# Projecting a tile one tile (one block) behind its transposes, in a four-layer graph network

## The chip, the cores and the metric

The kernel runs on one core of a Trainium2 chip. The metric is the device time of one execution in microseconds (us); smaller is better. A core has engines that each work through their own instructions in order and wait for one another through semaphores: PE (TensorE: matmuls; its weight loads are listed apart as PEld), ACT (ScalarE), DVE (VectorE) and POOL (GpSimd), and SP (SyncE), which here issues the DMAs.

## What is computed

A graph of 3327 nodes with 256 features each goes through four layers, each of the form x = x + layer(relu(layernorm(x)), adj). All data are float32. Layer 0 (two steps of attention with a top-p cut) is not touched by the change. Layers 1 to 3 are, cut to what matters:

```python
# layer 1
filt = tanh(adj * adj) * (adj > 0)               # the largest 700 of a row; rows here have fewer
x = x + relu(filt @ (tanh(h @ W_proj + b_proj) @ W_gcn) + b_gcn)
# layer 2
h = maximum(layernorm(x), 0)
Wh = h @ W
e = leaky_relu((Wh @ a[:256])[:, None] + (Wh @ a[256:])[None, :], 0.2)
x = x + softmax(where((adj > 0) | eye, e, -9e15), axis=1) @ Wh
# layer 3: the same with its own W and a, without eye, and elu around the product
```

Layer 2 so needs, for every node, the projection Wh of the normalized output of layer 1, and the two scores of Wh with the halves of a; layer 3 needs the same of layer 2's output.

## The kernel before

The 3327 nodes are padded to 26 tiles of 128 rows (NT = 26). A float32 product of two 128-row operands is two matmul instructions in the profile.

**Layer 1** is a loop over the tiles `it`. For each, the 26 blocks of the transposed adjacency come by DMA in two halves of 13 (`blk`, three tiles deep), DVE makes max(a, 0) * a in place (L1472), ACT the tanh in place (L1473), and PE multiplies the blocks with `gw`, 26 products that add up in a half of the PSUM tile `ps_wide` (L1476). One iteration later `summed(it - 1)` adds the bias, takes the relu and adds the residual on DVE (L1454, L1455; two tiles share one `ps_wide` and are done as a pair), and takes the layernorm statistics (L131 and L132 on DVE; L792, L793 and L1388 on POOL: adding epsilon, a power of -1/2, the product for the bias). Another iteration later `entered2(it - 2)` brings the tile into layer 2 by `Entry.tile_in`:

- ACT writes the normalized tile `hr` (L1394),
- PE transposes it in two halves into a `ps_row` (L785) and ACT copies that to `ht` (L786),
- PE multiplies `ht` with the weights and the two vectors made of them and `a` (L1399), into another `ps_row`,
- ACT copies the two scores to `sd` (L1403) and the rest to `wh` (L1404).

After the last tile of a span (four tiles; `ends`), `spread` transposes the scores of the span to a row (L1416, in a `ps_row`), ACT adds the `shift` and stores it in `dk` (L1419), POOL scales the scores (L1420), and DVE takes the largest of them for the first four rows of tiles (L1423). In the same iteration the rows of the adjacency of tile `it` come by DMA (`adj_rows`, L1488), DVE marks the positive ones in `pos` (L1490), POOL clears the padding (L1493), and SP stores it (L1494).

**Layers 2 and 3** are the function `attention`. It goes over seven spans of four tiles (the last has two) and, inside, over seven blocks `b` of four columns of tiles, two columns at a time: four exponentials on ACT (L1579, L1580), their maximum and the masking on DVE (L1581, L1582), and four tiles' products on PE (L1588). In blocks 1 to 4 the maximum over the next span's rows is taken (L1595), then turned into rows for the exponentials by transposes (L1535) and copies (L1538). At a span's end `finish` divides and adds the residual (L1611, L1629). The span's tiles enter layer 3 in the blocks of the next span: `todo` holds a list of work for each block, statistics two tiles ahead, then `tile_in`, and after the fourth tile the `spread`. For layer 3, `tile_in` also adds `wh` to `part` on POOL (L1407).

**What sets the order.** The program is written in the order of the loops; a scheduler then places each engine's instructions, and may move an instruction past others of the same engine. Buffers bound it: `hr` and `ht` have two, and `ps_row` has two for everything that uses it, taken in turn: transposes, projections, spreads, the rows of scores and the small product of `shift`. A new user of a `ps_row` waits until the one before the last has been copied out.

`Entry.__init__` also makes `shift` and `low` for its layer at once: DVE squares a column of weights (L1368), PE sums it with a matmul of ones (L1370), DVE (L1374) and POOL (L1375 to L1379) finish it. `entry2` is made before layer 1, `entry3` before layer 2.

Of the kernel before, what the change touches and what calls it, by code (L numbers as in the profile page):

```python
# [66 lines left out]
def kernel(  # L67
# [678 lines left out]
    def layers(fast):  # L746
# [606 lines left out]
        class Entry:  # L1353
# [5 lines left out]
            def __init__(self, name, w, wh, dk_tag, eye):  # L1359
                self.w, self.wh, self.eye, self.mv = w, wh, eye, {}  # L1360
                for t in wh.halves:
                    nc.gpsimd.memset(t[:, :, D : D + 1], 1.0)
                self.sd = late.tile([P, NT, 2], F32, name=f"sd{name}")
                self.d2 = late.tile([P, NT], F32, name=f"d2{name}")
                self.dk = slot(dk_tag, [P, NP], f"dk{name}")
                self.tops = late.tile([P, 4, len(spans)], F32, name=f"tops{name}")
                sq = late.tile([P, 2], F32, tag="sq", name="sq")
                nc.vector.tensor_tensor(sq, w[:, :, D + 1], w[:, :, D + 1], ALU.mult)  # L1368
                ps = ps_row()
                nc.tensor.matmul(ps[:, :2], ones, sq, start=True, stop=True)  # L1370
                self.shift = late.tile([P, 1], F32, name=f"shift{name}")
                self.low = late.tile([P, 1], F32, name=f"low{name}")
                shift = self.shift
                nc.vector.tensor_reduce(shift, ps[:, :2], AX.X, ALU.add)  # L1374
                nc.gpsimd.tensor_scalar(shift, shift, 1.01 * D, EPS, ALU.mult, ALU.add)  # L1375
                nc.gpsimd.tensor_tensor(shift, shift, half, ALU.pow)
                nc.gpsimd.tensor_scalar(shift, shift, 1.0, None, ALU.add)

                nc.gpsimd.tensor_scalar(self.low, shift, -1.0 + 2.0**-20, None, ALU.mult)  # L1379
                if not eye:  # L1380

                    self.part = late.tile([P, D + 1], F32, name="part")
                    nc.gpsimd.memset(self.part, 0.0)

# [5 lines left out]

            def tile_in(self, it, src):
                hr = late.tile([P, D], F32, tag="hr", bufs=2, name="hr")
                mv = self.mv.pop(it)
                nc.scalar.activation(hr, src, AF.Relu, bias=mv[:, 0:1], scale=mv[:, 1:2])  # L1394
                ht = late.tile([P, D], F32, tag="ht", bufs=2, name="ht")
                transposed(hr, ht)
                ps = ps_row()
# [49 lines left out]
        with tc.tile_pool(name="l1", bufs=2, reuse_waits="tile") as l1:  # L1447
# [9 lines left out]

            def entered2(it):
                entry2.tile_in(it, xn(it))
                if it in ends:  # L1460
                    entry2.spread(ends.index(it))

            for it in range(NT):
# [17 lines left out]
                if it >= 2:  # L1481
                    entered2(it - 2)
                ar = slot(f"e{it % 2}", [P, NP], "adj_rows")
# [11 lines left out]
            summed(NT - 1)  # L1495
            entered2(NT - 2)
            entered2(NT - 1)


# [10 lines left out]
        def attention(entry, finish, following=None):  # L1510
# [33 lines left out]
            for i, span in enumerate(spans):  # L1544
# [16 lines left out]
                for b, j0 in enumerate(range(0, NT, JB)):  # L1561
# [30 lines left out]
                    if 1 <= b <= len(ahead):  # L1592
# [6 lines left out]
                        if b == len(ahead):  # L1599
                            sb_next = scores_of(ahead, top)  # L1600
                    if b and todo:
                        for work in todo.pop(0):
                            work()
# [10 lines left out]
                if following is not None:  # L1614

                    stats = [lambda it=it: following.stats(it, xn(it)) for it in span]
                    rest = [lambda it=it: following.tile_in(it, xn(it)) for it in span]
                    todo += [stats[:2]] + [rest[k : k + 1] + stats[k + 2 : k + 3] for k in range(n)]
                    todo.append([lambda i=i: following.spread(i)])
            for works in todo:  # L1620
# [108 lines left out]
```

## Time and the profile before

| | us |
|---|---|
| three runs | 3114.98, 3118.21, 3117.26 |
| their median | 3117.26 |
| the profiled execution | 3111.67 |
| its span, first to last instruction | 3109.9 |
| layer 1's products (L1476), first and last start | 1998.1, 2351.4 |
| the products of layers 2 and 3 (L1588), first and last start | 2379.2, 3099.2 |
| stretch of layer 3, 2772 to 3100: PE, DVE, ACT busy of 328 | 316.90, 290.74, 243.73 |

Times in a timeline are microseconds from the start of the span; a group such as "x4" is four instructions in a row with the time from the first's start to the last's end. What stands in brackets at the end of a line is how long the engine stood idle before it, and the instruction that ended the wait. In the list of waits the columns are who waited for whom, the total in us, how often, and the longest. The mean granted PE clock of the execution is 0.973 of full speed.

### The profile page before, as it was taken

What the parts mean: (1) busy time and instruction counts of PE and PEld (TensorE: products, weight loads), DVE (VectorE), ACT (ScalarE), POOL (GpSimd) and SP (SyncE); (2) the same over time, 40 slices, a digit from 0 to 9 for tenths busy, and PEclk for the clock granted to TensorE, in tenths of its full rate; (3) what the DMA queues carried; (4) which work ended last, traced back from release to release, by engine and by line L of the source; (5) the groups of instructions that cost most, each with busy time, mean ns of one, the idle gap of its engine ahead of it and who ended that gap; (6) DMA issues with size and microseconds to landing.
All of it is one profiled execution on the core that took longest, in us unless ns stands there. A gap on an engine that the chain in (4) does not pass through costs nothing. (4 is left out here: it accounts for less than half of the span.)

```text
span 3109.9 us, 37662 instructions
## 1 busy us (share of the span) xinstructions
PE 2831.8 (91%) x13454; PEld 2278.7 (73%) x13454; DVE 2382.5 (77%) x4159; ACT 1968.2 (63%) x2607; POOL 375.5 (12%) x716
## 2 busy tenths in 40 slices
PE   7788899999999899999999988999997999979998
PEld 5466677777778577767777767788876787758887
DVE  3678888778873588888976868577765999769996
ACT  6767787768763666677665645333334776757776
POOL 0220010000001000000000014311120233210000
PEclk9899999999999999999999999999998999989999
DMA  4431112331242232211232232388861211112221
GB/s 137 131 102 51 55 42 77 91 89 49 70 119 88 76 97 60 59 43 51 73 89 79 76 110 75 111 315 313 321 228 33 71 59 57 31 49 78 72 76 38
DMA packets 183034, 298.83 MB, mean 96 GB/s; under 512 B 24700, under 2 KB 137015, under 8 KB 179511
## 3 DMA queue, kind: packets, MB, share of 16 engines
q1 hardware_dynamic: 182838, 296.34, 30.3%
q8 instruction: 108, 1.77, 0.2%
q14 instruction: 88, 0.72, 0.1%
HBM read 251.97 MB, written 44.30 MB: 95 GB/s over the span
## 5 line engine op out<-in xcount | busy, mean ns | idle before, releaser
L1121 ACT ACTIVATE junk_a<-e,minus 128x3328 int8<-128x3328 f32 x208 | 638.7, 3071 | 3.7
L1588 PE MATMUL ps_wide<-wh,places 128*128 128x257 f32 x1872 | 452.5, 384 | 35.9 <-DVE places L1582 34.8
L1588 PEld LDWEIGHTS ps_wide<-wh,places 128*128 128x128 f32 x1872 | 354.4, 192 | 94.5 <-ACT places L1580 16.5
L914 PE MATMUL ps_acc<-h,blk 128*128 128x258 f32 x1352 | 333.6, 399 | 44.5 <-ACT xf_row L922 35.3
L1011 DVE TENSOR_SCALAR_CACHE_REDUCE e<-ps_wide 128x1024 f32<-128x1024 f32 (+1 forms) x176 | 178.4, 1019 | 212.0 <-PE ps_wide L1037 211.5
L914 PEld LDWEIGHTS ps_acc<-h,blk 128*128 128x128 f32 x1352 | 262.1, 199 | 99.9 <-ACT xf_row L922 40.5
L914 PE MATMUL ps_acc<-xf,blk 128*128 128x256 f32 x1352 | 314.0, 384 | 13.0 <-ACT xf_row L922 13.0
L940 PE MATMUL ps_out<-h,wt 128*128 128x256 f32 x1352 | 312.6, 383 | 5.0 <-ACT wt L952 4.9
L940 PE MATMUL ps_out<-xa,wt 128*128 128x256 f32 x1352 | 312.6, 381 | 1.4 <-ACT wt L952 1.4
L1579 ACT ACTIVATE places<-places,sd 128x512 f32<-128x512 f32 (+1 forms) x364 | 246.6, 685 | 105.5 <-PE ps_wide L1588 72.3
L1476 PE MATMUL ps_wide<-gw,blk 128*128 128x256 f32 x1352 | 303.9, 382 | 0.2 <-ACT blk L1473 0.2
L914 PEld LDWEIGHTS ps_acc<-xf,blk 128*128 128x128 f32 x1352 | 254.1, 191 | 63.2 <-ACT xf_row L922 18.5
L1476 PEld LDWEIGHTS ps_wide<-gw,blk 128*128 128x128 f32 x1352 | 257.0, 192 | 35.1 <-ACT blk L1473 0.6
L940 PEld LDWEIGHTS ps_out<-h,wt 128*128 128x128 f32 x1352 | 250.8, 191 | 41.1 <-ACT wt L952 7.0
L940 PEld LDWEIGHTS ps_out<-xa,wt 128*128 128x128 f32 x1352 | 248.3, 190 | 34.9 <-ACT wt L952 3.7
L1126 DVE SCALAR_TENSOR_TENSOR below<-e,v 128x3328 f32<-128x3328 f32 x72 | 265.4, 3687 | 1.8
L1580 ACT ACTIVATE places<-places,d 128x512 f32<-128x512 f32 (+1 forms) x364 | 235.9, 682 | 46.1 <-DVE places L1581 45.7
L1581 DVE TENSOR_TENSOR places<-places,places 128x1024 f32<-128x1024 f32 (+1 forms) x182 | 210.4, 1164 | 67.8 <-ACT places L1579 65.8
L952 ACT COPY wt<-ps_wide 128x1024 f32<-128x1024 f32 x208 | 175.1, 846 | 88.1 <-PE ps_wide L950 87.4
L1037 PE MATMUL ps_wide<-keys,q 64*128 64x512 f32 (+1 forms) x832 | 214.8, 567 | 16.0 <-DVE e L1011 13.1
L1582 DVE SCALAR_TENSOR_TENSOR places<-blk_s,places 128x1024 f32<-128x1024 int8 (+1 forms) x182 | 206.1, 1141 | 2.0
L1020 ACT ACTIVATE e<-e,nm 128x3327 f32<-128x3327 f32 x44 | 134.8, 3064 | 85.3 <-DVE nm L1019 85.2
(274 smaller groups left out, 4314.8 us busy)
## 6 DMA issues: line engine op xcount, KB each, us to landing
blk<-in_adj_t SPq DMA_DIRECT2D x104, 448.0 KB, 3.4
blk<-in_adj_t SPq DMA_DIRECT2D x52, 832.0 KB, 6.8
adj_rows<-in_adj SPq DMA_DIRECT2D x25, 1663.5 KB, 8.1
blk<-in_adj_t SPq DMA_DIRECT2D x104, 384.0 KB, 3.3
blk_s<-sign_d SPq DMA_DIRECT2D x72, 256.0 KB, 2.9
blk_s<-pos_d SPq DMA_DIRECT2D x44, 416.0 KB, 3.6
pos_d<-pos SPq DMA_DIRECT2D x22, 416.0 KB, 2.8
xf_d<-xf_row SPq DMA_DIRECT2D x52, 128.0 KB, 2.4
```

Source lines behind the costliest of these rows:

```text
L914: nc.tensor.matmul(acc[:, :w], blk[:, j, :], xf(jc)[:, :w], start=(jc == 0), stop=(jc == NT - 1))
L940: nc.tensor.matmul(po, wt[:, k * P : (k + 1) * P], xa(jc)[:, :D], start=(jc == 0), stop=(jc == NT - 1))
L1011: nc.vector.tensor_scalar(e.rearrange("p (f c) -> p f c", f=2)[:, :, c0 : c0 + cw], pl.rearrange("p (f c) -> p f c", f=2)[:, :, :cw], 1.0, ...
L1037: nc.tensor.matmul(pl[:, f * 512 : f * 512 + cw], q[f * DA : (f + 1) * DA, :], kt[f * DA : (f + 1) * DA, s, c0 : c0 + cw], start=True, sto ...
L1121: nc.scalar.activation(junk, es[i], (AF.Relu, AF.Sign)[n], bias=minus[:, 0, i : i + 1], accum_out=(ga, sa)[n][:, 0, i : i + 1],)
L1126: nc.vector.scalar_tensor_tensor(below, es[i], v[:, 3, i : i + 1], es[i], ALU.is_ge, ALU.mult, accum_out=v[:, 1, i : i + 1],)
L1476: nc.tensor.matmul(po, filt[:, j * P : (j + 1) * P], gw(jc), start=(jc == 0), stop=(jc == NT - 1))
L1579: nc.scalar.activation(e1[:, :, q, :], s0, AF.Exp, bias=sd[:, jc + q, 1:2])
L1580: nc.scalar.activation(e2[:, :, q, :], s1, AF.Exp, bias=d2[:, jc + q : jc + q + 1])
L1581: nc.vector.tensor_tensor(e1, e1, e2, ALU.max)
L1582: nc.vector.scalar_tensor_tensor(e1, signs[:, :n, j : j + 2, :], 0.0, e1, ALU.is_gt, ALU.min)
L1588: nc.tensor.matmul(pos_[k], e1[:, k, q, :], wh(jc + q)[:, : D + 1], start=(jc + q == 0), stop=(eye and jc + q == NT - 1),)
```

## The change

`tile_in` is parted into `turned` (normalize, transpose, copy to `ht`) and `projected` (the projection and its copies). In layer 1 the loop calls `turned` for tile it - 2 as before, and `projected`, with the spread behind it, for tile it - 3. In layer 2 the list of a block holds `turned` of one tile and `projected` of the tile before; the fourth tile's projection stands with the spread in the last block. What made `shift` in the constructor is a method `shifted` of its own, called in iteration 2 of layer 1 for layer 2, and in the second span's second block of layer 2 for layer 3. The number of instructions of each kind is the same.

```diff
@@ -1357,19 +1357,25 @@
             def __init__(self, name, w, wh, dk_tag, eye):
-                self.w, self.wh, self.eye, self.mv = w, wh, eye, {}
+                self.w, self.wh, self.eye, self.mv, self.ht = w, wh, eye, {}, {}
                 for t in wh.halves:
                     nc.gpsimd.memset(t[:, :, D : D + 1], 1.0)
                 self.sd = late.tile([P, NT, 2], F32, name=f"sd{name}")
                 self.d2 = late.tile([P, NT], F32, name=f"d2{name}")
                 self.dk = slot(dk_tag, [P, NP], f"dk{name}")
                 self.tops = late.tile([P, 4, len(spans)], F32, name=f"tops{name}")
+                self.shift = late.tile([P, 1], F32, name=f"shift{name}")
+                self.low = late.tile([P, 1], F32, name=f"low{name}")
+                if not eye:
+                    self.part = late.tile([P, D + 1], F32, name="part")
+                    nc.gpsimd.memset(self.part, 0.0)
+            def shifted(self):
                 sq = late.tile([P, 2], F32, tag="sq", name="sq")
-                nc.vector.tensor_tensor(sq, w[:, :, D + 1], w[:, :, D + 1], ALU.mult)
+                nc.vector.tensor_tensor(sq, self.w[:, :, D + 1], self.w[:, :, D + 1], ALU.mult)
                 ps = ps_row()
                 nc.tensor.matmul(ps[:, :2], ones, sq, start=True, stop=True)
-                self.shift = late.tile([P, 1], F32, name=f"shift{name}")
-                self.low = late.tile([P, 1], F32, name=f"low{name}")
                 shift = self.shift
                 nc.vector.tensor_reduce(shift, ps[:, :2], AX.X, ALU.add)
                 nc.gpsimd.tensor_scalar(shift, shift, 1.01 * D, EPS, ALU.mult, ALU.add)
@@ -1377,10 +1383,6 @@
                 nc.gpsimd.tensor_scalar(shift, shift, 1.0, None, ALU.add)
                 nc.gpsimd.tensor_scalar(self.low, shift, -1.0 + 2.0**-20, None, ALU.mult)
-                if not eye:
-                    self.part = late.tile([P, D + 1], F32, name="part")
-                    nc.gpsimd.memset(self.part, 0.0)
             def stats(self, it, src):
@@ -1388,12 +1390,15 @@
                 nc.gpsimd.tensor_scalar(mv[:, 0:1], mv[:, 0:1], mv[:, 1:2], -1.0, ALU.mult, ALU.mult)
                 self.mv[it] = mv
-            def tile_in(self, it, src):
+            def turned(self, it, src):
                 hr = late.tile([P, D], F32, tag="hr", bufs=2, name="hr")
                 mv = self.mv.pop(it)
                 nc.scalar.activation(hr, src, AF.Relu, bias=mv[:, 0:1], scale=mv[:, 1:2])
-                ht = late.tile([P, D], F32, tag="ht", bufs=2, name="ht")
-                transposed(hr, ht)
+                self.ht[it] = late.tile([P, D], F32, tag="ht", bufs=2, name="ht")
+                transposed(hr, self.ht[it])
+            def projected(self, it):
+                ht = self.ht.pop(it)
                 ps = ps_row()
                 for c in range(2):
                     nc.tensor.matmul(
@@ -1455,8 +1460,8 @@
                 nc.vector.scalar_tensor_tensor(xn(it), pre, 0.0, xs(it), ALU.max, ALU.add)
                 entry2.stats(it, xn(it))
-            def entered2(it):
-                entry2.tile_in(it, xn(it))
+            def projected(it):
+                entry2.projected(it)
                 if it in ends:
                     entry2.spread(ends.index(it))
@@ -1479,7 +1484,11 @@
                 if it >= 1:
                     summed(it - 1)
                 if it >= 2:
-                    entered2(it - 2)
+                    entry2.turned(it - 2, xn(it - 2))
+                if it == 2:
+                    entry2.shifted()
+                if it >= 3:
+                    projected(it - 3)
                 ar = slot(f"e{it % 2}", [P, NP], "adj_rows")
                 r = rows_of(it)
                 if r < P:
@@ -1493,8 +1502,11 @@
                 nc.gpsimd.memset(pos[:, N:], 0)
                 nc.sync.dma_start(pos_d[it], pos)
             summed(NT - 1)
-            entered2(NT - 2)
-            entered2(NT - 1)
+            projected(NT - 3)
+            entry2.turned(NT - 2, xn(NT - 2))
+            projected(NT - 2)
+            entry2.turned(NT - 1, xn(NT - 1))
+            projected(NT - 1)
         att = fast.enter_context(tc.tile_pool(name="att", bufs=1, reuse_waits="tile"))
@@ -1598,6 +1610,8 @@
                         )
                         if b == len(ahead):
                             sb_next = scores_of(ahead, top)
+                    if following is not None and (i, b) == (1, 1):
+                        following.shifted()
                     if b and todo:
                         for work in todo.pop(0):
                             work()
@@ -1614,9 +1628,12 @@
                 if following is not None:
                     stats = [lambda it=it: following.stats(it, xn(it)) for it in span]
-                    rest = [lambda it=it: following.tile_in(it, xn(it)) for it in span]
-                    todo += [stats[:2]] + [rest[k : k + 1] + stats[k + 2 : k + 3] for k in range(n)]
-                    todo.append([lambda i=i: following.spread(i)])
+                    turned = [lambda it=it: following.turned(it, xn(it)) for it in span]
+                    made = [lambda it=it: following.projected(it) for it in span]
+                    todo += [stats[:2]] + [
+                        turned[k : k + 1] + made[max(k - 1, 0) : k] + stats[k + 2 : k + 3] for k in range(n)
+                    ]
+                    todo.append(made[-1:] + [lambda i=i: following.spread(i)])
             for works in todo:
                 for work in works:
                     work()
```

## The prediction, made before the changed kernel had run

> **What bounds the kernel now.** I read the page first, then the granted clock and busy time by stretches, then the waits of TensorE (PE), then the order of time on PE and ScalarE (ACT) around the longest wait.
>
> ```profile
> span 3109.9 us, 37662 instructions
> PE 2831.8 (91%) x13454; PEld 2278.7 (73%) x13454; DVE 2382.5 (77%) x4159; ACT 1968.2 (63%) x2607; POOL 375.5 (12%) x716
> ...
> 2041.00:2352.00 311.00, 294.06 (x1360) 253.39 (x1358) 201.55 (x229) 101.79 (x141) 52.37 (x94) 0.98 0.76 278
> 2372.00:2745.00 373.00, 342.94 (x1564) 289.09 (x1564) 328.17 (x436) 261.64 (x484) 109.77 (x102) 0.97 0.18 56
> ```
>
> The columns of the last two lines are the stretch, its length, busy time of PE, PEld, DVE, ACT and POOL, PE clock, DMA share and GB/s. Layer 1 (first line) is a PE loop: DVE and ACT stand idle for a third and two thirds of it. In layer 2 (second line) DVE is busy 88% beside PE's 92%: two engines share the bound. So a PE wait is worth its length in layer 1, and only part of it in layer 2. PE's waits, layer 1 first, then the main ones of layer 2 (total us, times, longest):
>
> ```profile
> PE ps_row L1399 <- ACT ht L786: 19.2, 11, 5.0
> PE ps_row L785 <- ACT hr L1394: 3.4, 1, 3.4
> ...
> PE ps_wide L1588 <- DVE places L1582: 17.3, 9, 8.5
> PE ps_row L785 <- ACT hr L1394: 6.6, 2, 5.7
> PE ps_row L1399 <- ACT ht L786: 4.5, 7, 2.1
> ```
>
> In layer 1 nearly all of PE's waiting is the wait that the change moves: the projection (L1399) for ACT's copy of the transposes (ht, L786). PE's order of time shows an undisturbed pair of tiles and the worst one:
>
> ```profile
> 2109.50 0.38 PE L785 MATMUL ps_row<-ident,hr 128*128 128x128 f32 x2
> 2121.82 0.38 PE L785 MATMUL ps_row<-ident,hr 128*128 128x128 f32 x2
> 2134.13 0.38 PE L785 MATMUL ps_row<-ident,hr 128*128 128x128 f32 x2
> ...
> 2281.27 0.38 PE L785 MATMUL ps_row<-ident,hr 128*128 128x128 f32 x2
> 2281.48 1.03 PE L1476 MATMUL ps_wide<-gw,blk 128*128 128x256 f32 x4
> 2287.53 2.09 PE L1399 MATMUL ps_row<-w2l,ht 128*128 128x258 f32 x4 [5.02 <-ACT ht L786]
> ```
>
> A tile takes (2134.13 - 2109.50) / 2 = 12.315 us when nothing waits. At 2281 the transposes are done, only four matmuls stand between them and the projection (0.87 us of cover), and PE then waits 5.02 us although both blocks of the tile it is in are ready (their tanh ended by 2269.1). Why ACT is late:
>
> ```profile
> 2283.65 0.60 ACT L1394 ACTIVATE hr<-xs,mv_a 128x256 f32<-128x256 f32 x1 [10.60 <-POOL pos L1493]
> 2284.16 3.05 ACT L1473 ACTIVATE blk<-blk 128x1664 f32<-128x1664 f32 x2
> 2287.11 0.36 ACT L786 ACTIVATE ht<-ps_row 128x256 f32<-128x256 f32 x1
> ```
>
> The copy is third in a queue whose head waits for POOL. PE pays for a tanh (L1473) whose result it needs only a tile later.
>
> [...] the ht copy, free to run at 2281.6, starts at 2287.11 behind the hr and the two tanh. [...] after the 5.02 us wait (the projection's four matmuls take 2.09 instead of 1.03 us, the next 48 take 12.58 instead of 10.52) [...] after the 1.94 us wait at 2190 the 20 us around it have a mean clock of 0.91. [...] the power on POOL (L793) takes 0.57 us alone and 5.48 us at 2276.63 beside DVE's memset and block arithmetic. That is why the hr above was late.
>
> **The change, part by part.**
>
> *Layer 1, the loop.* Nothing is added or taken away; per tile two transposes, the projection and its copies stay. As built, PE's order becomes tile's 52 matmul passes (26 products), transposes of tile it-2, projection of tile it-3, with ht copied a whole tile (about 12 us) before. From the first loop transposes (2041.64) to the last (2351.66) PE took 310.0 us. Undisturbed it is 23 tiles x 12.315 = 283.2, plus five spreads of d at 0.57 (four transposes, 2136.09 to 2136.66) = 2.9, so 286.1. The excess, 310.0 - 286.1 = 23.9 us, is all that the loop can give: 16.95 of waits for ht (3.00, 0.90, 0.94, 2.85, 1.94, 0.69, 1.61, 5.02) and about 7 of slow clock and restart after them.
>
> What is late next? The blocks. Setting each tile's second-last tanh against PE's start of that tile, the smallest slack is 8.9 us (tile 4), later 13 to 26. Even with the tanh where they are now, PE could come forward by 16.4 us at tile 22 (start 2302.0, tanh ready 2285.7) and keep it. Loads of blocks follow PE's release of buffers, so they come forward too; DMA, at 0.83 to 0.89 of its engines in this stretch, has room for 7% more rate. Supply alone therefore leaves between 16.4 and 23.9.
>
> One wait stays. PSUM's ps_row has two buffers. At the five tiles with a spread (it = 6, 10, 14, 18, 22) the spread takes the buffer of the transposes just made, so PE still waits there for this tile's ht, with 0.87 us of cover as now. In the trace before such a wait hit those places with 2.85 (it = 10) and 1.61 (it = 18) us. Lower bound nothing, since the spread's four DVE reductions (L1423, 2.5 us) now stand behind the next rows' pos on DVE and statistics come earlier; upper bound three waits of about 2.7 = 8. I take 4. Layer 1's loop: 23.9 - 4 = 20.
>
> *Moved setup.* The shift (one DVE product, one small matmul, one DVE reduce, four POOL operations) leaves the heads of both layers. The 128x2 matmul took 0.28 us; DVE's reduce for layer 3 waited 8.02 us at 2365.61 but freed the DVE 0.1 us before the dk it needs next. Gain 0.2. At its new places a wait of DVE for that matmul lies behind a block product that ends later (2043.6) than the matmul would (about 2042.3), so costs nothing.
>
> *Layer 1's end.* One more projection (0.87) stands after the last products, but before transposes that waited 3.41 us for hr: nothing.
>
> *Layer 2, the spans.* PE's ht waits in the loop are 0.16 three times, 2.13 and 0.48; the 2.13 at 2618 also costs about 1.8 of slow clock (ten passes in 3.96 instead of 2.17). Sum 4.9. But they lie in or near the half of each span in which PE waits for DVE anyway (1.91, 1.11, 1.79, 2.40, 0.89 us at the same place of other spans), so DVE's places end the wait next. Against this, a span's fourth projection now stands after its last product and the spread directly behind: three transposes and one product (0.8 us) cover ACT's sd copy, which comes about 1.2 us after the projection's start, or later behind one exponential (0.67). That is up to 1.1 us for five spans, in the same half that waits for DVE. Bounds +5.5 and -4.9; I take a gain of 0.5. POOL's adds of part (L1407) and d2 follow sd and nobody waits for them; SP issues the same transfers, pos stores and row loads changing places by one.
>
> *Layer 2's end.* The last product no longer stands behind the projection of the tile before (0.87), and the last two tiles' transposes both stand before both projections, so the second starts when the first ends (2749.40 + 1.88 = 2751.28) instead of 2752.45: 1.2. Together 2.1, of which I take 1.5, since ACT, POOL and DVE steps lie between.
>
> Sum: 20 + 0.2 + 0.5 + 1.5 = 22 us. The profiled execution took 3111.67 (its span 3109.9), 5.6 below the median 3117.26; so 3089.7 for an execution like it and 3117.26 - 22 = 3095 for the median.
>
> **Rivals.**
>
> *The wait moves to the spreads or to the supply.* For it: ACT still holds tanh behind ht and hr, POOL still stalls on pos stores (up to 8.3 us). Against it: only five of 23 tiles have a spread. It leaves half of layer 1's gain, 10 to 12 in all: 3106.
>
> *The order does not matter.* The built schedule might find PE waiting for hr or blocks by the same amount. Against it: the slacks above, and hr never held PE inside this loop. Within 6 us: 3117.
>
> *Layer 2's span boundary makes it slower.* ACT, in order, must copy sd after the last projection of a span before its next exponentials. If it lost a full round each time (two exponentials 1.33, DVE's maximum and minimum 1.22 + 1.14) plus a slow clock of 1.8, that is 5.5 x 6 boundaries = 33, less 22: 3128. It decides from (22 + 6.2) / 6 = 4.7 us a boundary. Against it: ACT already waits there for PE (1.23 us before sd, 1.30 before the next exponentials).
>
> *Layer 2 gains as well.* If exponentials run ahead once ht is free: 5 to 9 more, 3088.
>
> **How the numbers follow.** Forecast (3090 to 3102) 0.55; half of it 0.20; layer 2 too 0.10; no change 0.08; slower 0.07. About 0.2% (6.2 us) is what a measurement can tell from none. Faster is 0.55 + 0.20 + 0.10 = 0.85. The range runs from layer 2's gain in full (3085) to the lower end of half the gain (3109).
>
> **What would show it.** Right: layer 1's waits of the projection for ht near zero, tiles 12.3 apart, ht waits only at spreads, layer 2's length within 4 us of now. Wrong: PE waiting in layer 1 for tanh or hr, or span boundaries of layer 2 longer than 57 us.

## The result, and the profile after

| kernel | median (lowest to highest, runs) | profiled execution, its span |
|---|---|---|
| before | 3117.74 us (3112.79 to 3121.76, 8) | 3111.67, 3109.9 |
| changed | 3101.58 us (3097.76 to 3110.83, 8) | 3099.39, 3097.6 |

The ratio is 0.9950 (95% interval 0.9937 to 0.9962): 15.6 us faster, between 11.8 and 19.6. The forecast was 3095 (3085 to 3109). The page's first lines, and then busy time by stretches (the stretch, its length, busy time of PE, PEld, DVE, ACT and POOL, PE clock, DMA share, GB/s), of the changed kernel:

```profile
span 3097.6 us, 37705 instructions
...
PE 2821.7 (91%) x13454; PEld 2275.3 (73%) x13454; DVE 2383.9 (77%) x4159; ACT 1966.5 (63%) x2607; POOL 371.6 (12%) x716
```

```profile
2041.00:2343.00 302.00, 290.72 (x1356) 253.19 (x1355) 201.17 (x231) 100.68 (x138) 38.03 (x99) 0.98 0.77 286
...
2370.00:2735.00 365.00, 339.55 (x1566) 288.97 (x1566) 323.11 (x436) 253.08 (x473) 113.37 (x108) 0.98 0.19 57
```

Both stretches are shorter, with the same work in them but for one projection (four matmuls, 0.87 us), which now falls behind layer 1's stretch. Setting the two executions stage by stage: up to layer 1's first transposes in its loop 0.64 us less; layer 1's loop, from these to its last transposes, 301.8 (2041.00 to 2342.76) against 310.0; from there to layer 2's first score transposes 17.2 against 17.1; layer 2, up to layer 3's score transposes, 386.3 against 390.0; the rest 351.3 against 351.2. The gain of 12.3 in these two executions is 8.2 in layer 1's loop (some 0.6 of it that projection: the loop's first tile now has none and takes 11.67) and 3.7 in layer 2. (The median gained 16: the profiled execution of before was 6.1 below its own median, that of the changed kernel 2.2.)

The waits of PE in the changed kernel, layer 1 first (2040 to 2340 us), then the main ones of layer 2 (2360 to 2746.2 us):

```profile
PE ps_row L1421 <- ACT sd L1408: 7.3, 3, 3.2
PE ps_row L1421 <- ACT ht L786: 4.0, 1, 4.0
...
PE ps_wide L1600 <- DVE places L1594: 16.0, 7, 8.5
PE ps_acc L1600 <- DVE places L1594: 6.7, 3, 2.9
PE ps_row L785 <- ACT hr L1396: 4.7, 2, 4.1
PE ps_row L1421 <- ACT sd L1408: 3.7, 4, 1.3
```

The projection (now L1404) waits for ht nowhere in layer 1's loop: eight waits of 16.95 us are gone. But 11.3 us of waits stand at the spread (now L1421), in four of its five places. PE's order of time at two of them:

```profile
2089.62 0.38 PE L785 MATMUL ps_row<-ident,hr 128*128 128x128 f32 x2
2089.83 1.04 PE L1404 MATMUL ps_row<-w2l,ht 128*128 128x258 f32 x4
2094.88 0.90 PE L1421 MATMUL ps_row<-ident,sd 128*128 128x128 f32 x3 [4.01 <-ACT ht L786]
2095.57 1.92 PE L1481 MATMUL ps_wide<-gw,blk 128*128 128x256 f32 x4
2097.28 0.42 PE L1421 MATMUL ps_row<-ident,sd 128*128 128x128 f32 x1
2097.49 12.25 PE L1481 MATMUL ps_wide<-gw,blk 128*128 128x256 f32 x48
...
2202.30 0.65 PE L1421 MATMUL ps_row<-ident,sd 128*128 128x128 f32 x4 [3.17 <-ACT sd L1408]
2202.79 13.08 PE L1481 MATMUL ps_wide<-gw,blk 128*128 128x256 f32 x52
```

After the waits of 4.01 and 3.17 the products run slower (48 passes in 12.25 us, 52 in 13.08; 52 take 11.38 when nothing was waited for); the granted clock was 0.50 from 2094.18 to 2101.01 and 0.51 from 2203.41 to 2206.82. Waits and slow clock together are all that this loop has over an undisturbed one, which is 285.5 us here (286.1 less 0.65, since the first tile, without a projection, takes 11.67 and not 12.32): 301.8 - 285.5 = 16.3 us, of which 11.3 wait and 5.0 slow clock. ScalarE ahead of the first of these places, and VectorE, which it waits for:

```profile
2092.96 1.59 ACT L1478 ACTIVATE blk<-blk 128x1664 f32<-128x1664 f32 x1 [4.90 <-DVE blk L1477]
2094.46 0.37 ACT L786 ACTIVATE ht<-ps_row 128x256 f32<-128x256 f32 x1
2094.76 1.59 ACT L1478 ACTIVATE blk<-blk 128x1664 f32<-128x1664 f32 x1
2096.26 0.14 ACT L1408 COPY sd<-ps_row 128x2 f32<-128x2 f32 x1
```

```profile
2087.50 3.62 DVE L1499 TENSOR_SCALAR_CACHE_REDUCE pos<-adj_rows 128x3327 uint8<-128x3327 f32 x1 [2.28 <-DMA adj_rows<-in_adj]
...
2091.04 3.69 DVE L1477 SCALAR_TENSOR_TENSOR blk<-blk 128x1664 f32<-128x1664 f32 x2
```

The queue that made ht late before the change is still there. The ht copy, free to run once the transposes of 2089.62 were done (2090.00), starts at 2094.46, behind a tanh that waits 4.90 for its block; the block's product waits on VectorE behind pos; pos waited 2.28 for its rows' load. (At the other three places the head of ScalarE's queue is an hr that waited 6.79 us for its statistics on GpSimd, and tanh that waited 2.55 and 1.73 for VectorE.) And sd, the 128x2 copy that the spread is made of, stands behind ht and a second tanh and starts at 2096.26. Before the change PE met this queue at the projection, and when ht came, sd followed at once. Now PE passes the projection and meets the queue at the spread.

### The profile page after: what moved, and what is told of

Same layout as the page of the kernel before. It is cut to its first block, busy times and chain, and to the rows that moved or that the text cites. A ratio compares the mean times of both kernels' runs of the same rounds, so it can differ in the third digit from the quotient of the medians.

```text
span 3097.6 us, 37705 instructions
## 1 busy us (share of the span) xinstructions
PE 2821.7 (91%) x13454; PEld 2275.3 (73%) x13454; DVE 2383.9 (77%) x4159; ACT 1966.5 (63%) x2607; POOL 371.6 (12%) x716
## 5 line engine op out<-in xcount | busy, mean ns | idle before, releaser
L1481 PE MATMUL ps_wide<-gw,blk 128*128 128x256 f32 x1352 | 301.2, 383 | 0.8 <-ACT blk L1478 0.8
L1171 DVE MAX8 w<-below 128x8 f32<-128x3328 f32 x52 | 188.3, 3621 | 0.3
```

The costliest lines, as they stand in the source:

```text
L1171: nc.vector.max(w9[:, i, 1:9], below)
L1481: nc.tensor.matmul(po, filt[:, j * P : (j + 1) * P], gw(jc), start=(jc == 0), stop=(jc == NT - 1))
```

## The experiments

All twelve runs, with what can be compared across them: the stretch of layer 1 from the transposes that follow tile 3's products to those that follow tile 25's (273.8 us when nothing waits, the spreads included; some 0.6 to 1.5 less where the spread is later or the order deeper: a later spread costs 0.45 instead of 0.57, and in the deeper order one projection falls outside), PE's waits inside it, and the median. Profiled columns are from one execution each.

| kernel | stretch, us | PE waits in it | median, us | ratio to before (95%) |
|---|---|---|---|---|
| before | 297.7 | 16.9 | 3113.6 to 3117.7, measured anew beside the others | |
| changed | 290.1 | 11.3 | 3101.58 | 0.9937 to 0.9962 |
| l1_only | 288.0 | 10.1 | 3102.40 | 0.9941 to 0.9969 |
| l2_only | 295.0 | 14.3 | 3111.55 | 0.9982 to 1.0002 |
| before_memset_dve | 297.0 | 14.9 | 3110.94 | 0.9973 to 0.9995 |
| own_buffer | 289.5 | 11.2 | 3100.51 | 0.9933 to 0.9962 |
| memset_dve | 286.2 | 8.9 | 3097.55 | 0.9919 to 0.9952 |
| spread_late | 285.6 | 9.4 | 3098.49 | 0.9934 to 0.9965 |
| deeper_only | 290.4 | 12.8 | 3099.51 | 0.9921 to 0.9953 |
| deeper_late | 278.3 | 5.0 | 3088.45 | 0.9891 to 0.9922 |
| deeper_late_memset | 280.6 | 5.7 | 3086.87 | 0.9889 to 0.9925 |
| deeper_own | 280.7 | 6.8 | 3090.47 | 0.9895 to 0.9926 |
| deeper_far | 278.6 | 4.0 | 3091.49 | 0.9908 to 0.9934 |
| deeper_far_own | 274.3 | 1.4 | 3082.25 | 0.9891 to 0.9924 |

How far single executions scatter in this stretch shows where two kernels have the same layer 1: changed and l1_only lie 2.1 us apart, before and l2_only 2.7. A difference of that size between two rows says nothing by itself.

**Which layer gave what.** Layer 1's part alone, with layer 2 as before (l1_only):

```diff
-                    turned = [lambda it=it: following.turned(it, xn(it)) for it in span]
-                    made = [lambda it=it: following.projected(it) for it in span]
...
+                    rest = [lambda it=it: (following.turned(it, xn(it)), following.projected(it)) for it in span]
+                    todo += [stats[:2]] + [rest[k : k + 1] + stats[k + 2 : k + 3] for k in range(n)]
+                    todo.append([lambda i=i: following.spread(i)])
```

And layer 2's part alone, with layer 1 as before (l2_only):

```diff
                     entry2.turned(it - 2, xn(it - 2))
-                if it == 2:
-                    entry2.shifted()
-                if it >= 3:
-                    projected(it - 3)
+                    projected(it - 2)
```

Expected of l1_only:

> The change in layer 1 alone; layer 2 as in the kernel before (the projection of a tile in the step of its transposes, the spread a step after the last projection). From the two profiles layer 1's loop gave 8.2 us and layer 2 3.7 (0.8 in its spans, 2.8 at its end). If the parts add: this is 3105 to 3109 us (about 8 below before), and layer 2, from its first score transposes to layer 3's, takes 389 to 391 us as before (389.98; the changed kernel 386.3). If layer 2's gain is only the scatter of that stage: 385 to 388 us there, and a median as the changed kernel's, near 3101.

Expected of l2_only:

> The change in layer 2 alone; layer 1 as in the kernel before. If the parts add: 3110 to 3114 us (about 3.7 below before), layer 1's loop 307 to 312 us from its first to its last transposes, layer 2 385.5 to 387.5. If layer 2 gives nothing: 3114 to 3118, layer 2 389 to 391. The rival that layer 2's span boundary costs time: above 3118.

Measured: 13.4 us below before for layer 1's part (9.7 to 18.4 by the interval of its ratio), 4.2 for layer 2's (from 0.6 slower to 5.6 faster). The first met the second branch of its expectation (3102.4, and 388.0 us in layer 2), the second its first branch (3111.55, loop 307.3, and 384.8 in layer 2, even below what was expected). Two single executions can't settle 3 us. Over all profiles layer 2 took 390.0, 389.5 and 388.0 us with the old order, and 384.6 to 389.4 (eleven, mean 387.3) with the new one: a gain of 1.9. Most of the change's gain is layer 1's.

**Buffer or data.** The prediction had the remaining wait at the spread down to the ring of two PSUM buffers. This run gives the spread a buffer of its own, and leaves the order as it is:

```diff
-            def spread(self, i):
+            def spread(self, i, ps_of=None):
...
-                pb = ps_spread()
+                pb = (ps_of or ps_spread)()
...
-                    entry2.spread(ends.index(it))
+                    entry2.spread(ends.index(it), ps_acc)
```

> The changed kernel, with layer 1's spread of d written into a PSUM buffer of its own (the acc buffer, unused in this layer) in place of the ring of two; layer 1's loop alone is touched. In the changed kernel PE waits 11.3 us ahead of four spreads. Theory A (the spread waits for its data: the sd copy stands on ScalarE behind this tile's ht copy, and both behind a tanh or an hr): no change, loop 300 to 303 us from its first to its last transposes as against 301.8, spread waits 10 to 12, median 3098 to 3104. Theory B (it waits for the ring buffer, as the prediction had it): the waits shrink to below 3, loop 290 to 293, median 3088 to 3093.

PE's order of time in that run, at the same place:

```profile
2091.41 0.49 PE L1421 MATMUL ps_acc<-ident,sd 128*128 128x128 f32 x3
...
2097.02 0.47 PE L1421 MATMUL ps_acc<-ident,sd 128*128 128x128 f32 x1 [4.26 <-ACT sd L1408]
```

Three of the four transposes now run at once, since their sd are older; the fourth needs the sd of the projection just ahead of it and waits 4.26. Four such waits sum to 10.4 us, the loop takes 301.2, the median is 3100.51. Theory A: the spread waits for data; the buffer alone costs nothing that stands out from the scatter.

**GpSimd's wait for a store.** Two runs move one instruction, in the changed kernel and in the kernel before:

```diff
-                nc.gpsimd.memset(pos[:, N:], 0)
+                nc.vector.memset(pos[:, N:], 0)
```

Expected of memset_dve:

> The changed kernel, with the memset of pos' last byte on VectorE in place of GpSimd. GpSimd then no longer waits for the store of pos ahead of the next tile's statistics. Theory D (hr at the head of ScalarE's queue, held by GpSimd's wait for that store, is what makes ht and sd late): spread waits fall from 11.3 to below 4, loop below 294, median 3089 to 3094. Theory E (the heads of the queue wait for VectorE and for loads: a tanh for its block, an hr for statistics queued behind pos): spread waits 8 to 12, loop 299 to 303, median 3097 to 3104.

Expected of before_memset_dve:

> The kernel before, with the same memset moved to VectorE. Its eight waits of the projection for ht sum to 16.95 us, and the longest (5.02) followed an hr put down to the memset on GpSimd. Theory D: the waits fall below 6, loop (310.0) below 297, median 3100 to 3106. Theory E: the waits stay at 11 to 18, loop 303 to 311, median 3110 to 3120.

In the changed kernel the waits fell from 11.3 to 8.9 and the median to 3097.55, both as theory E had them; the loop, 297.9, lies between the two theories, 3.9 below the changed kernel's and 1.8 below that of l1_only. In the kernel before the waits stayed at 14.9, with the longest, behind the same queue, at 4.8 instead of 5.0, and the loop at 309.4. So a memset on GpSimd that waits for a store is not what most of the waits come from, and in the longest it had no part, though the bracket named it. ScalarE and GpSimd there, with the memset on VectorE:

```profile
2284.54 0.60 ACT L1394 ACTIVATE hr<-xs,mv_a 128x256 f32<-128x256 f32 x1 [10.61 <-POOL mv_a L1388]
```

```profile
2277.51 5.48 POOL L793 TENSOR_TENSOR mv_a<-mv_a,minus_half 128x1 f32<-128x1 f32 x1
2283.09 1.42 POOL L1388 TENSOR_SCALAR mv_a<-mv_a 128x1 f32<-128x1 f32 x1
```

The hr waits as long as before, for statistics whose power takes 5.48 us as before; the memset in the bracket of the kernel before only stood right behind these statistics on GpSimd (2283.55). That is the reason that the prediction gave beside its bracket. Of the other four long waits in the kernel before, at three a tanh that waited for VectorE (5.89, 6.11 and 3.39 us) stands ahead of ht, and VectorE waits for rows (28.9 us in nine waits in this loop) and blocks (17.1 in eight) from memory.

**The spread later.** Half a tile, some 6 us:

```diff
             def projected(it):
                 entry2.projected(it)
+
+            def spread(it):
                 if it in ends:
                     entry2.spread(ends.index(it))
...
+                    if hb == 0 and it >= 4:
+                        spread(it - 4)
```

> The changed kernel, with layer 1's spread of d issued in the middle of the next tile, after its first 13 products (about 6 us later). Theory A (the spread waits for sd, late on ScalarE): the waits at the spreads go, with the slow clock behind them; loop 287 to 291 us (286.1 undisturbed, 301.8 in the changed kernel), median 3087 to 3091. Rival C (the blocks' supply limits the loop: what PE wins it loses again waiting for a tanh): loop 296 to 302, PE waits at products for blk instead, median 3096 to 3102.

The waits at the spreads went (0.45 left), but the loop took 297.3 us (2040.95 to 2338.24), and the median, 3098.49, is 3 below the changed kernel's, which the ratios to before don't tell apart: both in rival C's range. The waits have new places: 7.1 us at the transposes two tiles behind, and 1.8 of a projection for dk, through the ring. At the longest, PE, ScalarE, VectorE and GpSimd around it:

```profile
2206.07 0.38 PE L785 MATMUL ps_row<-ident,hr 128*128 128x128 f32 x2
...
2224.26 0.69 PE L785 MATMUL ps_row<-ident,hr 128*128 128x128 f32 x2 [5.72 <-ACT hr L1396]
```

```profile
2223.61 0.60 ACT L1396 ACTIVATE hr<-xs,mv_a 128x256 f32<-128x256 f32 x1 [10.32 <-POOL mv_a L1390]
```

```profile
2205.64 3.62 DVE L1503 TENSOR_SCALAR_CACHE_REDUCE pos<-adj_rows 128x3327 uint8<-128x3327 f32 x1 [3.62 <-DMA adj_rows<-in_adj]
...
2213.44 3.62 DVE L1503 TENSOR_SCALAR_CACHE_REDUCE pos<-adj_rows 128x3327 uint8<-128x3327 f32 x1
...
2216.98 0.75 DVE L1459 TENSOR_TENSOR pre<-ps_wide,bg 128x256 f32<-128x256 f32 x2
```

```profile
2219.23 1.76 POOL L792 TENSOR_SCALAR mv_a<-mv_a 128x1 f32<-128x1 f32 x1 [6.47 <-DVE mv_a L132]
2221.08 2.13 POOL L793 TENSOR_TENSOR mv_a<-mv_a,minus_half 128x1 f32<-128x1 f32 x1
```

Read upwards from PE: the transposes wait for hr, hr for its statistics on GpSimd, these for VectorE, where the sums of two tiles (pre) stand behind two pos, the first of which waited 3.62 us for its rows, with a block product and the spread's four reductions between the two. The statistics on GpSimd take 3.9 us more. It is rival C in that the wait came back, but not for a block: one more link of the chain has too little distance.

**One tile deeper.** The next runs give the chain another tile, without the later spread, with it, and with the memset moved as well:

```diff
-                if it >= 2:
-                    entry2.turned(it - 2, xn(it - 2))
+                if it >= 3:
+                    entry2.turned(it - 3, xn(it - 3))
...
-                if it >= 3:
-                    projected(it - 3)
+                if it >= 4:
+                    projected(it - 4)
```

The later spread, in the two kernels that have it, is that of the run above, a tile on:

```diff
+                    if hb == 0 and it >= 5:
+                        spread(it - 5)
```

Expected of deeper_late, then of deeper_late_memset, and, with the results of these known, of deeper_only:

> The changed kernel with layer 1 one tile deeper: transposes three tiles behind the products in place of two, the projection four, the spread in the middle of the tile after that. With the spread moved alone, PE waited 5.7 and 1.4 us for hr: the statistics of a pair of tiles stood on VectorE behind two pos that waited for row loads. Theory F (slack of one tile in each step of the chain is what lacks): from tile 3's products' end to tile 25's 274 to 278 us (273.8 undisturbed, 290.1 in the changed kernel), waits of PE below 3, median 3084 to 3090. Rival C (the supply of rows and blocks limits the loop, and each wait that is removed comes back further on): 282 to 290 us, with PE waiting for blk, hr or ht for 6 or more, median 3094 to 3102.

> The same, with the memset of pos' last byte on VectorE, so that GpSimd's statistics never wait for a store. If what is left in the run with the deeper order comes from GpSimd's wait for the store: 2 to 4 us less than that run (the memset alone brought 4 us in layer 1's loop of the changed kernel, 301.8 to 297.9). Under theory F nothing is left for it: the same as the deeper order within 2 us. Under rival C the same too.

> The changed kernel with layer 1's transposes and projections one tile deeper (three and four tiles behind the products), but the spread directly behind the projection, as in the changed kernel. With the deeper order and the later spread together the stretch from tile 3's to tile 25's products' end fell from 290.1 to 278.3 us, with the later spread alone only to 285.6. Theory G (two separate needs: the spread needs distance from its projection, the transposes distance from their statistics): the spreads wait 6 to 11 us for sd or ht as in the changed kernel, no wait for hr; stretch 284 to 290, median 3094 to 3101. Rival H (depth alone does it, because copies then run ahead on ScalarE): spread waits below 4, stretch 276 to 281, median 3086 to 3091.

Depth alone changes nothing in the stretch (290.4; PE waits at two spreads alone, 5.9 and 6.9 us):

```profile
2110.83 0.90 PE L1421 MATMUL ps_row<-ident,sd 128*128 128x128 f32 x3 [5.88 <-ACT ht L786]
...
2219.64 0.90 PE L1421 MATMUL ps_row<-ident,sd 128*128 128x128 f32 x3 [6.88 <-ACT ht L786]
```

The brackets name ht, which frees the ring's buffer. But sd, which the fourth transpose needs, comes on ScalarE behind ht and a second tanh (2112.21 and 2221.03), so a buffer alone should have moved these waits and not ended them; that was not tried. The later spread alone brings 4.5, both together 11.8 (278.3), and 13 us of the median: 3088.45. That is theory G, two needs of which each hides the other's gain, though the waits (12.8) and the stretch of deeper_only came out just above what it gave. Theory F had the median, missed the stretch by little (278.3 against 274 to 278) and had the waits too low (5.0 against below 3). With the memset moved too, nothing is added (3086.87, and 280.6 in the stretch, within the scatter).

**The last waits.** What was left are one or two waits for sd, for ht or for dk, the spread's copy, through the ring. A buffer of its own for the spread (deeper_own), another tile of distance for it (deeper_far), and then both (deeper_far_own). Set against deeper_late:

```diff
-                    entry2.spread(ends.index(it))
+                    entry2.spread(ends.index(it), ps_acc)
```

```diff
-                    if hb == 0 and it >= 5:
-                        spread(it - 5)
+                    if hb == 0 and it >= 6:
+                        spread(it - 6)
```

> The deeper order with the later spread, and the spread in a PSUM buffer of its own. What was left there were waits of a spread for ht (2.5) and sd (1.0), and of two projections for the spread's copy dk (1.5 in all), which reuse of the ring of two causes but for the sd. Expected: the waits for dk and for ht at the spread go, 1 to 2 us of waits stay; stretch 274 to 277.5 us, median 3083 to 3088. If the ring is not what is left: stretch 278 to 281, median 3087 to 3091.

> The deeper order with layer 1's spread another tile later (in the middle of the second tile after its projection, some 18 us behind it, as against 6). What was left with the deeper order: the spread near 2217 us waited 2.5 us for ht and 1.0 for sd, and with a buffer of its own 6.8 for sd, whose copy stood on ScalarE behind a tanh that waited 5.6 us for its block. If distance covers that: no wait for sd at the spreads, waits of PE below 3 in all, stretch from tile 3's to tile 25's products' end 274 to 278 us (278.3 with the deeper order), median 3083 to 3088. If the late block is what binds there (rival C): the same wait of 3 to 7 us at the same place for another cause (ht, dk or blk), stretch 278 to 282, median 3087 to 3091.

> The deeper order with the spread 18 us behind its projection and in a PSUM buffer of its own: each of the two alone left one wait of PE of 4.0 us (a projection for dk, through the ring) or 6.8 us (the spread for sd). If both needs are met and nothing else binds: no wait above 1 us, stretch from tile 3's to tile 25's products' end 274 to 276.5 us (273.8 undisturbed), median 3083 to 3088. Under rival C (what is left is the late blocks, and the wait only moves): a wait of 2 to 6 us for ht, hr or blk near the same place, stretch 277 to 281, median 3087 to 3092.

The first two missed what was hoped of them (280.7 and 278.6), each with one long wait, for sd and for dk. deeper_own met its other branch; deeper_far met it in the stretch, with a median 0.5 above it and the wait at another place, near 2184 us, where the branch had it near 2217:

```profile
2218.44 0.48 PE L1421 MATMUL ps_acc<-ident,sd 128*128 128x128 f32 x1 [6.77 <-ACT sd L1408]
```

```profile
2183.87 1.68 PE L1404 MATMUL ps_row<-w2l,ht 128*128 128x258 f32 x4 [4.03 <-ACT dk L1424]
```

ScalarE's order of time in deeper_own ahead of the first of these is the one of the changed kernel over again:

```profile
2214.95 1.59 ACT L1480 ACTIVATE blk<-blk 128x1664 f32<-128x1664 f32 x1 [5.57 <-DVE blk L1479]
2216.45 0.37 ACT L786 ACTIVATE ht<-ps_row 128x256 f32<-128x256 f32 x1
2216.75 1.59 ACT L1480 ACTIVATE blk<-blk 128x1664 f32<-128x1664 f32 x1
2218.25 0.14 ACT L1408 COPY sd<-ps_row 128x2 f32<-128x2 f32 x1
```

With both, the stretch is 274.3, as expected, and one wait of 1.4 is left in it, where none above 1 was expected:

```profile
2212.41 1.14 PE L1404 MATMUL ps_row<-w2l,ht 128*128 128x258 f32 x4 [1.42 <-ACT wh L1409]
```

The late block is there in this run too (the tanh at 2208.64 waited 5.90), and all that PE notices is this 1.4: the projection's buffer in the ring comes free with the copy wh, which stands on ScalarE behind that tanh, ht and a second tanh. So rival C falls for this loop: the supply makes the queues late, but it does not limit the loop; with distance at every link and a buffer of its own for the spread PE runs all but through. The median, 3082.25, is the lowest, 19 us below the changed kernel; but before was low beside it too (3113.57), and by the ratio to before deeper_far_own isn't told from deeper_late. That it beats the other deeper kernels rests on the stretch, of one execution each. Against the changed kernel the profiles show where the gain comes from: 15.8 in the stretch (290.1 to 274.3; 0.9 of it the projection that now stands behind it), and 3.8 between the last tile's transposes and layer 2's score transposes (17.2 to 13.4), where one more tile's transposes and projection fill the wait for the last hr.

## The prediction, step by step

*What it said of the cause.* Right in the main: PE's waits for ht in layer 1 were the loss, ScalarE's queue makes them, and the order one tile behind takes them away: 16.95 us of waits of the projection are gone. Of the queue's head it showed one example and gave GpSimd's slow statistics as its reason; before_memset_dve bears that out for this wait, but at three of the other four long ones the head is a tanh that waits for VectorE.

*Layer 1's loop, +20 forecast, 8.2 in the profile.* The step that failed is "One wait stays ... I take 4", with bounds of 0 and 8: the excess left is 16.3 us, 11.3 of waits at four spreads and 5.0 of slow clock, nearly all after two of them. Three things in it were wrong. The waits were priced at what before showed at these tiles (2.85 and 1.61), but before, the projection just ahead had already waited for the same queue, and the spread found sd at its door; with that wait gone the spread is the first to meet the queue, in four places of five. The cause was put to the ring's buffer; it is the sd of the projection directly ahead, as own_buffer shows, and that sd stands on ScalarE behind ht and a tanh. And slow clock was counted for the old waits and not for the new ones. This is the first rival's mechanism ("the wait moves to the spreads or to the supply"), given 0.20; in the loop its half of the gain, about 10, is nearer to the 8.2 than the 20 of the forecast. That 20 was there to be had is shown by deeper_far_own, whose stretch is 297.7 - 274.3 = 23.4 below before, 0.9 of it the projection outside. The prediction's own sign of being right, tiles 12.3 apart, failed at four tiles, which took 14.4 to 20.0 us.

*Supply.* "Supply alone leaves between 16.4 and 23.9" held: no wait of PE for a block was seen in the loop in any run. But the supply does set how late ScalarE's and VectorE's queues run, and that the argument by slack of the tanh did not see. That the DMA had room for 7% more rate was an estimate from the share in the profile; no run tried it.

*The moved setup, 0.2.* Not tried by itself. The shift's matmul is at 2041.22 in layer 1's loop and is followed by products without a wait.

*Layer 1's end, 0.* Held: 17.2 us against 17.1 in the two profiles.

*Layer 2, +0.5 in the spans and +1.5 at the end.* The sum, 2.0, held (1.9 over eleven profiles with the new order against three with the old); the two terms did not. From the first to the last score transposes of the layer the new order takes 311.5 on average against 309.2, a loss of 2.3 where a gain of 0.5 was taken (the loss was bounded by 5.5), with spread waits for sd of up to 1.3 where the bound had 1.1. A sign of being wrong was a span longer than 57 us; from score transposes to score transposes one took 58.9, but in the kernel before one took 57.7 already, so the sign could not tell. From the last score transposes to layer 3's first it takes 75.9 (74.5 to 76.8) against 80.0 in each old one, a gain of 4.1 where 1.5 was taken. Part of it is the end itself, before and then after:

```profile
2741.55 0.60 PE L1416 MATMUL ps_row<-ident,sd 128*128 128x128 f32 x4
2747.84 0.69 PE L785 MATMUL ps_row<-ident,hr 128*128 128x128 f32 x2 [5.68 <-ACT hr L1394]
2749.40 2.09 PE L1399 MATMUL ps_row<-w3l,ht 128*128 128x258 f32 x4 [0.88 <-ACT ht L786]
2751.28 0.63 PE L785 MATMUL ps_row<-ident,hr 128*128 128x128 f32 x2
2752.45 2.09 PE L1399 MATMUL ps_row<-w3l,ht 128*128 128x258 f32 x4 [0.53 <-ACT ht L786]
```

```profile
2731.99 0.73 PE L1421 MATMUL ps_row<-ident,sd 128*128 128x128 f32 x4
2736.79 0.69 PE L785 MATMUL ps_row<-ident,hr 128*128 128x128 f32 x2 [4.06 <-ACT hr L1396]
2738.09 0.69 PE L785 MATMUL ps_row<-ident,hr 128*128 128x128 f32 x2 [0.61 <-ACT hr L1396]
2738.57 3.65 PE L1404 MATMUL ps_row<-w3l,ht 128*128 128x258 f32 x8
```

From the last product's end to layer 3's score transposes it is 17.2 us before (2741.55 to 2758.70) and 15.2 after (2731.12 to 2746.31): 2.0, although one more projection (0.87) now stands in this part. The prediction had 1.2 for it, from both pairs of transposes standing ahead of the projections, which now follow each other without a wait; hr also comes 0.6 earlier after the last product (5.7 us against 6.3). The rest of the 5.3 in this pair lies in the span ahead: a projection stands behind the last product instead of ahead of it (0.9), and waits for hr and ht (0.88 and 0.48) are gone, with one of 1.05 for places in their stead. What makes up the remaining 2 us was not followed further.

*The range and the whole.* 3101.58 lies in the likeliest case's own range only just (3090 to 3102). The loop gave 12 less than forecast, layer 2 what was forecast. That the median still came to lie there is in part luck: taken off the forecast's base of 3117.26, the 12.3 us of the two profiles give 3105, nearer to the first rival's 3106 than to 3095. The median gained 4 more than the profiles, since the profiled execution of before was a fast one; where the slower executions of before spend those 4 us stays open.

## What to carry to other kernels

When a wait is moved off an instruction, look at what is behind it on the same engine and needs anything from the queue that was late: a copy that used to be ready because PE had waited already becomes the next wait. Give every link of such a chain its distance (statistics to transposes, transposes to projection, projection to spread), and its own buffer where a ring ties two links together; with one link short, each cure alone shows under a third of the gain or none (spread later 4.5 us of the stretch, depth 0, own buffer 0.6, of which 2 to 3 can be scatter; all together 15.8). Before a late head of ScalarE's queue is shortened, move its consumers further from it: with all of that in place a tanh that had waited 5.90 us cost PE 1.4 (deeper_far_own). One cure was not tried: to place ht and sd ahead of the tanh in ScalarE's order, so that they never stand behind a late block.

## What the runs showed of the hardware

How much slow clock follows a wait is not set by the wait alone. In layer 1's loop every single wait of 3.10 us or more was followed by 1.5 to 3.2 us of further loss. So were waits of 1.94 (before), 2.08 (memset_dve) and 2.57 (before_memset_dve), but after those of 2.42 (own_buffer), 2.67 (changed), 2.85 and 3.00 (before) it was 0.3 or less. The granted PE clock was at half speed (0.50 to 0.51) four times in the loops of before and of the changed kernel: from 2191.15 to 2194.56 (3.41 us) and from 2286.72 to 2293.55 (6.83) in before, from 2094.18 to 2101.01 (6.83) and from 2203.41 to 2206.82 (3.41) in the changed kernel. The two starts lie 95.57 us apart in before and 109.23 in the changed kernel, 28 and 32 times 3.413. Laid out in windows of that length, counted from these starts, before's waits of 3.00 and 1.94 look so (columns as above):

```profile
2054.62:2058.03 3.41, 1.44 (x7) 0.94 (x5) 3.41 (x7) 0.89 (x1) 0.00 (x0) 1.00 0.66 199
2058.03:2061.44 3.41, 2.38 (x11) 2.11 (x12) 3.02 (x7) 0.98 (x2) 2.08 (x2) 1.00 0.96 367
2187.74:2191.15 3.41, 1.48 (x7) 0.98 (x6) 3.41 (x6) 2.79 (x3) 0.00 (x0) 1.00 1.07 320
2191.15:2194.56 3.41, 3.41 (x12) 2.69 (x11) 1.79 (x6) 2.10 (x5) 2.23 (x7) 0.50 0.95 396
```

The longer wait is split over two windows, 1.97 and 1.03 us; the shorter lies nearly whole in one, and the next runs at half speed. Of the full-speed windows in these two loops, those followed by one at half speed had PE idle for 1.93 and 3.41 us (before) and for 3.31 and 2.31 (changed); the most idle of the others had 1.97 and 1.92 (before), so that idle time in one window goes with the slow clock that follows, but does not settle it near 1.9. In the loops of all fourteen profiles a single wait of less than 1.9 us was followed by at most 0.3 us of further loss; the wait of 1.94 cost 1.8 on top, about half of the window at half speed.

GpSimd's two small operations on mv_a took 1.76 and 2.13 us beside VectorE's block products in spread_late, and 0.22 and 0.57 beside its pos (2190.76 and 2191.06 in the same run). No run shows whether it is VectorE's work that makes the difference, nor what in it.

Where layer 0 ends scatters: in the six runs of the deeper order, with the same work ahead, the transposes that follow tile 3's products came between 2050.2 and 2059.4 us, so that differences of some us between two single executions are read from the stretch concerned and not from the span.
